# Order of layer 2's last block, place of a Tanh, ties and weight sums in a four-layer graph kernel

## The chip, the cores and the metric

The kernel runs on one core of one Trainium2 chip. The metric is the device time of one execution in microseconds (us). Three executions were timed, and the median is quoted; one more was profiled.

## What is computed

128 graphs of 64 nodes with 512 features pass four layers; after each, the input is added and the rows are normalised. Everything is 32-bit float. The reference, cut to what matters:

```
# layer 0: hypergraph convolution, twice (H = adj != 0)
h = relu(conv(x, adj, W1, b1)); h = layer_norm(h, gamma, beta); x = norm(x + conv(h, adj, W2, b2) + x)
# layer 1: attention from a sum of two scores
s = (x @ w) @ a
A = s[..., :, None] + s[..., None, :]
A = tanh(A / 8) * 8;  A = where(A >= 0, A, 0.1 * A);  A = exp(A) * adj
A = A / A.sum(-1) * adj.sum(-1);  x = norm(x + A @ x @ w)
# layer 2: three graph convolutions
h = relu(adj @ (x @ W1) + b1); h = relu(adj @ (h @ W2) + b2); x = norm(x + adj @ (h @ W3) + b3)
# layer 3: attention with 8 heads, adjacency and distance terms, output projection
attn = softmax(q k^T * scale) * 0.33 + 0.33 * adj + 0.33 * exp(-adj)
x = norm(x + (attn @ v) @ W_out + b_out)
```

## The kernel before

**Groups and steps.** The graphs are cut into 16 groups of 8 (512 rows: four pairs of graphs, 128 rows each). Three streams of work run at once. In step s, stream "a" does layers 0 and 1 of group s (`first_half`), stream "b" layer 2 and the first part of layer 3 of group s-1 (`second_half`), and stream "t" the rest of layer 3 of group s-2. Group 0 has its own code for layers 0 and 1 (`first_group`). Three strings, `order`, `step_1` and `step_last`, name the pieces of one step in the order in which they are written down: `b.l2c1` is the piece of stream b up to the `yield "l2c1"`. Steps 2 to 15 use `order`. From that sequence a scheduler sets the order of the instructions on each engine; it may move them, except where `behind(key)` ties an instruction after one that was remembered in `last_add` under that key (`tc.issue_after`), or where an engine is strict (the start, and the end).

**One multiplication.** `multiply` (L546) computes a 512x512 by 512x512 product with seven products of quarter blocks instead of eight. Each is one call of `product`: four matmul instructions of 128x256 (eight rows of the trace), twice that where two left sides are added. They run with the weights B11, T1, T2, B21, T3, B22, T4, where T1 to T4 are sums and differences of weight blocks (L263 to L268). There are three PSUM accumulators. `a_` takes B11, T2, T3 and T4; between them its contents are copied out by `snap` (L555): u1 after B11, u2 after T2. `b_` takes T1 (copied as u5) and B22. `c_` takes B21 alone. VectorE then adds: c + u1 (L575), a after T3 + u5 (L581), b after B22 + u2 (L590). T4 may write `a_` only when L581 has read it; T3 only when u2 has been copied. The last quarter is copied after T4 (L600, or L602 with a residual). The copies of u run on ScalarE, or on VectorE with a residual (`res`). `stops` says after which products the piece ends.

**Layer 2's last block.** Stream b's third multiplication has the key `l2c_q`, its result is g; 16 matmuls `agg` (L1145) follow, which need all of g, and VectorE adds them to x (L1151). Two of its adds are tied by `held`: c + u1 behind `e_(q+1)` and b + u2 behind `t_(q+1)`, both of layer 1.

**Layer 1's attention weights** run beside it, for group q+1: VectorE makes the scores (L815), transposes them (L620, L624), adds (L822, key `e`); ScalarE does Tanh (L825), VectorE the leaky part (L826), ScalarE Exp (L827), VectorE two products (L829, L830), the sum and its reciprocal (L834, L835), the same transposes again, and the last product (L838, key `t`). Tanh needs another table of functions than the root before it, so a table load stands ahead of it in ScalarE's order. `graph_T` then multiplies t with x (`gt_l`, L481), and two engines or ScalarE alone (`both`) copy the result out (L490, L492) for layer 1's multiplication `l1w`, whose T1 needs a sum of it, `s_l` (L518).

**The projection** of stream t has the key `wo_q` and a residual: pieces o1 (B11), o2 (T1), o3 (T2), and the rest. In o2 and o3 it is tied behind products 5 and 7 of `l2c_(q+1)`.

**Weights.** A ring of 20 tiles is filled by DMAs on SP's queue some 20 products ahead. For group 0 the sums T1 to T4 of a weight are made on VectorE (`making`, `make_half` for two parts of it) and stored by POOL's queue for the later groups.

Of the kernel before, what the change touches and what calls it, by code (L numbers as in the profile page):

```python
# [8 lines left out]
FP = mybir.dt.float32  # L9
# [32 lines left out]
def kernel(  # L42
# [455 lines left out]
    def newest(engine):  # L498
        return next(i for i in reversed(nc.cur_bb.bb.instructions) if i.engine == engine)

    def behind(key):
        return tc.issue_after(last_add[key]) if key in last_add else nullcontext()
# [25 lines left out]
    def product(acc, lefts, wt_q, what, first, last, flipped):  # L528
        ws = stream.take(*wt_q, what)
        n_k = 2 * len(lefts)  # L530
        for blk in range(2):
            for i in range(n_k):
                left, wt = lefts[i // 2].left[what][:, i % 2], ws[i // 2][:, i % 2]
                if flipped:
                    lhsT, rhs = wt[:, blk * P : (blk + 1) * P], left
                else:
                    lhsT, rhs = left[:, blk * P : (blk + 1) * P], wt

                ten.matmul(  # L539
                    acc[:, blk, :], lhsT, rhs,  # L540
                    start=(first and blk == 0 and i == 0), stop=(last and i == n_k - 1),
                    skip_group_check=True,
                )
        stream.done(*wt_q, what)

    def multiply(lefts, wt_q, dst, key, flipped=False, res=None, stops=(3,), then=None, held={}):  # L546

        acc = [ps_acc.tile([P, 2, Q], FP, name=f"{n}_{key}", tag="acc") for n in "ab"]

        def snap(ps, m, n, what):
            t = work.tile([P, 2, Q], FP, name=f"{what}_{key}", tag="w")
            last_add[f"{key}.{what}"] = (act.copy(t, ps) if res is None else vec.tensor_add(t, ps, res(m, n))).ins  # L555
            return t

        pa, pc = acc
        product(pa, lefts, wt_q, B11, True, False, flipped)
        s1 = snap(pa, 0, 0, "u1")  # L560
        if 1 in stops:
            yield
        product(pc, lefts, wt_q, T1, True, False, flipped)
        s5 = snap(pc, 1, 1, "u5")
        if 2 in stops:
            yield
        product(pa, lefts, wt_q, T2, False, False, flipped)
        s2 = snap(pa, 0, 1, "u2")
        last_add[f"{key}.p3"] = newest(PE)
        if 3 in stops:  # L570
            yield
        pb = ps_acc.tile([P, 2, Q], FP, name=f"c_{key}", tag="acc")
        product(pb, lefts, wt_q, B21, True, True, flipped)
        with behind(held.get(4)):
            vec.tensor_add(dst(0, 0), pb, s1)  # L575
        if then:
            then(0, 0, dst(0, 0))
        if 4 in stops:
            yield
        product(pa, lefts, wt_q, T3, False, False, flipped)  # L580
        last_add[f"{key}.d"] = vec.tensor_add(dst(1, 1), pa, s5).ins  # L581
        if then:
            then(1, 1, dst(1, 1))
        last_add[f"{key}.p5"] = newest(PE)
        if 5 in stops:
            yield
        product(pc, lefts, wt_q, B22, False, True, flipped)
        last_add[f"{key}.p6"] = newest(PE)
        with behind(held.get(6)):
            last_add[key] = vec.tensor_add(dst(0, 1), pc, s2).ins  # L590
        if then:
            then(0, 1, dst(0, 1))
        if 6 in stops:
            yield
        product(pa, lefts, wt_q, T4, False, True, flipped)
        last_add[f"{key}.p7"] = newest(PE)
        if then:
            then(1, 0, pa)
        elif res is None:
            act.copy(dst(1, 0), pa)  # L600
        else:
            vec.tensor_add(dst(1, 0), pa, res(1, 0))  # L602

    def whole(gen):
        for _ in gen:
            pass

    def nat(t):

        return lambda m, n: t[:, 2 * m : 2 * m + 2, n * Q : (n + 1) * Q]  # L610
# [130 lines left out]
    def first_half(g):  # L741
# [65 lines left out]
        next(gen)  # L807
        yield "w21"
        whole(gen)
        layer_norm(xg, f"l0_{q}")  # L810

        s4 = small.tile([P, G], FP, name=f"s4_{q}", tag="s4")
# [8 lines left out]
        t = grp.tile([P, G, C], FP, name=f"t_{q}", tag="t", bufs=1)  # L821
        last_add[f"e_{q}"] = vec.tensor_add(t, e, bcast(s4, G)).ins  # L822
        yield "w2"
        with behind("l2c_0.u2") if q == 1 else nullcontext():
            act.activation(t, t, AF.Tanh, scale=0.125)  # L825
        vec.scalar_tensor_tensor(t, t, 0.1, t, ALU.mult, ALU.max)  # L826
        last_add[f"exp_{q}"] = act.activation(t, t, AF.Exp, scale=8.0).ins  # L827
# [12 lines left out]
        left = Left(f"l1_{q}")  # L840
        for duo in range(2):
            with behind("agg_0.p") if q == 1 else nullcontext():
                graph_T(pair, t, left.t, duo, f"l1_{q}", both=q > 1)
        yield "c3"
        with behind(f"wo_{q - 2}"):
            left.sums()
# [216 lines left out]
    def second_half(g):  # L1063
# [26 lines left out]
        h1.sums()  # L1090
        yield "l2a"
        g2 = big.tile([P, G, D], FP, name=f"g2_{q}", tag="big")
        for _ in multiply([h1], (w_g[1], q), nat(g2), f"l2b_{q}"):
            yield "l2b1"
        yield "l2b"
        adt = grp.tile([P, G, C], FP, name=f"adt_{q}", tag="adt", bufs=1)
# [27 lines left out]
        if not alone:  # L1124
# [1 line left out]
        h2.sums()  # L1126
        yield "gh"
        g3 = big.tile([P, G, D], FP, name=f"g3_{q}", tag="big")
        gen = multiply([h2], (w_g[2], q), nat(g3), f"l2c_{q}", stops=(3, 5),
            held={4: f"e_{q + 1}", 6: f"t_{q + 1}"})  # L1130
        next(gen)
        yield "l2c1"
        next(gen)
        yield "l2c2"
        whole(gen)
        yield "l2c"
        for duo in range(2):

# [68 lines left out]
        left.sums()  # L1207
        yield "osum"
        gen = multiply([left], (w_o, q), nat(xg), f"wo_{q}", res=nat(xg), stops=(1, 2, 3))
        next(gen)  # L1210
        yield "o1"
        for n in range(2):
            with behind(f"l2c_{q + 1}.p{5 + 2 * n}"):
                next(gen)
            yield f"o{n + 2}"
        whole(gen)
        yield "o"
        with behind(f"q_{q + 1}"):
# [166 lines left out]
    def taken(duo, ps, left):  # L1385
# [11 lines left out]
    """.split()  # L1397
    order = """
        t.v1 a.c1 t.v b.gt t.soft a.w1a1 a.w1a t.soft2 a.resid b.l2a1 b.l2a a.w1b1 t.ptp a.w1b t.pv a.lnh b.l2b1
        t.osum a.c2a b.l2b a.c2b b.gb3 load a.w21 b.gh a.w2 rows b.l2c1 b.l2c2 a.ss a.den b.l2c t.o1 t.o2 t.o3 a.c3 b.agg rows2 t.o  # L1400
        rows3 a.p1 b.xT a.p2 b.q1 a.ln1 b.q t.ln3 b.k1 prep b.k b.dots
    """.split()

    step_1 = """
        b.l2a1 b.l2a a.lnh b.l2b1 a.c2a b.l2b a.c2b b.gb3 load a.w21 b.gh a.w2 rows b.l2c1 b.l2c2 a.ss a.den sumsq b.l2c b.agg
        sumsq2 a.c3 a.p1 b.xT sumsk a.p2 b.q1 a.ln1 b.q rows2 b.k1 b.k prep b.dots
    """.split()

    step_last = """
        t.v1 b.gt t.v t.soft t.soft2 b.l2a1 t.ptp b.l2a t.pv t.osum b.l2b1 b.l2b b.gb3 b.gh b.l2c1 b.l2c2 b.l2c t.o1 b.agg  # L1410
        t.o2 t.o3 t.o b.xT b.q1 b.q t.ln3 b.k1 b.k b.dots
    """.split()
    rest_last = "t.v1 t.v2 t.v t.pv0 t.o1 t.pv1 t.o".split()
    orders = {1: step_1, NGRP: step_last, NGRP + 1: rest_last}
# [43 lines left out]
    for n, (who, q, name) in enumerate(todo):  # L1458
        if n == n_start:
            strict.clear()  # L1460
        if n == n_end:
            strict.update((PE, DVE))
        if who == "load":
            if q > 1:
                groups[q] = load_group(q)
        elif who == "rows":
            if q > 0:
                preps[q] = prepare(groups[q])
            with behind(f"l0w2_{q - 1}.d") if q > 1 else nullcontext():
                next(preps[q])  # L1470
        elif who in ("prep", "rows2", "rows3"):
            next(preps[q])
        elif who == "doubled":
            doubled(groups[q])
        elif who == "constant":
            constant(groups[q])
        elif who == "keep":
            wt = (*w_1, w_2, w_l1)[q]
            stream.keep(wt)
        elif who == "wa":  # L1480
            if isinstance(wa_parts, tuple):
                wa_parts = make_wa(*wa_parts)
                vec.tensor_copy(mcol, mcol8)
                vec.tensor_copy(mi, mi8)
            else:
                spread_wa(wa_parts)
        elif who == "rest":
            with in_turn(SP, POOL):
                wa_parts = load_wa()
                b2_bc = load_row(b2, D, "b2_bc")  # L1490
                groups[1] = load_group(1)
                load_atx(first)
                load_masks(first)
                load_masks_cols()
                gb1_col = load_col(gb1, KD, "gb1_col")
                gb2_col = load_col(gb2, KD, "gb2_col")
                gb3_bc = load_row(gb3, D, "gb3_bc")
                bo_bc = load_row(bout, D, "bo_bc")
        elif who in ("sumsq", "sumsq2"):
            stream.make_half(w_q)  # L1500
        elif who == "sumsk":
            stream.make(w_k, 0)
        elif who == "bw":
            next(bw_parts)
        else:
            side = "a" if who == "a" else "b"
            if (side, q) not in gens:
                gens[side, q] = (second_half if side == "b" else first_half if q > 0 else first_group)(groups[q])
            did = next(gens[side, q])
            assert did == name, (did, name)  # L1510
# [55 lines left out]
```

## Time and profile before

| | |
|---|---|
| median of 3 executions | 2749.85 us (2749.43 to 2751.62) |
| the profiled execution | 2749.3 us |
| its span, first to last instruction | 2747.5 us |
| mean granted TensorE clock | 0.999 |
| one step, from 692.24 to 861.00 (third a_l2c product) | 168.76 us |
| DMA, share of 16 engines, main queue | 47.5% |
| ScalarE's table loads for Tanh, each | 1.28 us |
| add on VectorE of 128x512 (L575 and the like) | 0.68 us, the next one starts 0.60 later |
| copy on ScalarE of 128x512 (L555) | 0.57 to 0.59 us |

The span of the profile is one execution from its first to its last instruction; the execution's own time is 1.8 us longer. In a line of the timeline stand the start and the duration in us, the engine (PE is TensorE, DVE is VectorE, ACT is ScalarE), the line of the kernel, the operation, what it writes and reads (names of tiles without numbers, so that `u_l2c` stands for u1, u5 and u2), and in brackets how long the engine was idle before it and what released it. The end of a matmul is modelled, so successive starts say more than durations.

### The profile page before, as it was taken

The page shows a single profiled execution, that of the slowest core. Times are in us where ns is not written, and L with a number is a line of the kernel's source. Part 1 is how long each engine was busy: PE and PEld are TensorE (multiplying, and loading weights), DVE is VectorE, ACT ScalarE, POOL GpSimd, SP SyncE. Part 2 cuts the span into 40 slices and gives each one's busy share as a digit, 9 for nine tenths or more (in the row PEclk, how much of TensorE's full clock was granted, in tenths as well). Part 3 has the DMA queues.
Part 4 walks back from the last instruction along what each step waited for, and adds up shares of the span by engine and source line. Part 5 has one row for each costly group of instructions (what it writes and reads, how often), then busy time and mean ns, then how long its engine had stood idle before and what let it go on. Part 6 is the DMA issues. An engine that isn't in the chain of part 4 may idle for free.

```text
span 2747.5 us, 67717 instructions
## 1 busy us (share of the span) xinstructions
PE 2722.5 (99%) x28770; PEld 2347.5 (85%) x28770; DVE 2079.6 (76%) x4117; ACT 803.3 (29%) x1444; POOL 38.1 (1%) x71
## 2 busy tenths in 40 slices
PE   9999999999999999999999999999999999999998
PEld 7878888888888888888888888888888888888887
DVE  6878687776877778777786877778777687776766
ACT  3323323233232322322223232232322323232232
POOL 2000000000000000000000000000000000000000
PEclk9999999999999999999999999999999999999999
DMA  8535454454544545445454454545545455454441
GB/s 264 179 107 164 129 166 140 141 165 131 171 132 138 167 132 165 131 143 167 130 167 131 143 165 131 165 126 153 159 131 170 129 159 147 130 163 132 151 124 61
DMA packets 309388, 405.14 MB, mean 147 GB/s; under 512 B 57408, under 2 KB 185184, under 8 KB 309088
## 3 DMA queue, kind: packets, MB, share of 16 engines
q1 hardware_dynamic: 304256, 385.58, 47.5%
q0 software_dynamic: 4832, 15.24, 1.5%
q8 instruction: 228, 3.74, 0.6%
q14 instruction: 72, 0.59, 0.1%
HBM read 369.78 MB, written 30.93 MB: 146 GB/s over the span
## 4 chain that ended last, share of the span: by engine, by line
PE 88%; DVE 10%; ACT 1%; issue 1%; POOL 0%; DVEq 0%; POOLq 0%
PE a_l0w L539 13%; PE b_l0w L539 7%; PE a_l2b L539 4%; PE a_q L539 4%; PE a_k L539 4%; PE a_l2a L539 4%; PE a_v L539 4%; PE c_l0w L539 4%; PE a_l1w L539 4%; PE gt_l L481 3%; PE a_wo L539 3%; PE gt_l0h L481 2%; PE a_l2c L539 2%; PE b_l2b L539 2%; PE b_q L539 2%; PE b_k L539 2%
## 5 line engine op out<-in xcount | busy, mean ns | idle before, releaser
L539 PE MATMUL a_l0w<-w2w,aT_l0h 128*128 128x256 f32 x720 | 164.3, 381 | 0.0
L457 DVE BATCH_NORM_STATS2 st_l<-x 128x6 f32<-128x512 f32 x244 | 157.4, 671 | 0.6
L539 PEld LDWEIGHTS a_l0w<-w2w,aT_l0h 128*128 128x128 f32 x720 | 135.6, 190 | 18.8
L463 DVE TENSOR_SCALAR x<-x,mv_l,rs_l 128x512 f32<-128x512 f32 x244 | 119.2, 541 | 2.2
L539 PE MATMUL b_l0w<-w2w,s_l0h 128*128 128x256 f32 x480 | 108.5, 379 | 0.0
L771 ACT ACTIVATE h<-h 128x1024 f32<-128x1024 f32 (+1 forms) x58 | 54.9, 947 | 178.5 <-DVE h L590 157.5
L539 PEld LDWEIGHTS b_l0w<-w2w,s_l0h 128*128 128x128 f32 x480 | 91.1, 190 | 12.5
L1120 ACT ACTIVATE aT_h<-gth,gb_col 128x256 f32<-128x256 f32 x128 | 48.4, 489 | 159.0 <-PE gth L1112 159.0
L492 ACT COPY aT_l<-gt_l 128x512 f32<-128x512 f32 x148 | 78.1, 597 | 56.8 <-PE gt_l L481 56.8
L447 ACT ACTIVATE rs_l<-mv_l,eps_t 128x4 f32<-128x4 f32 (+1 forms) x64 | 19.0, 297 | 255.9 <-DVE mv_l L458 244.2
L555 DVE TENSOR_TENSOR u_l0w<-a_l0w,b_bc 128x512 f32<-128x512 f32 x56 | 38.6, 688 | 69.3 <-PE a_l0w L539 69.3
L539 PE MATMUL a_l2c<-gwcw,aT_h 128*128 128x256 f32 x360 | 86.7, 384 | 4.2 <-ACT u_l2c L555 3.2
L539 PE MATMUL a_l2b<-gwbw,aT_h 128*128 128x256 f32 x360 | 86.6, 383 | 0.7 <-ACT aT_oT L1388 0.7
L539 PE MATMUL a_q<-aT_xT,wqw 128*128 128x256 f32 x360 | 85.1, 379 | 0.6 <-ACT aT_xT L1170 0.6
L539 PE MATMUL a_l1w<-ww,aT_l 128*128 128x256 f32 x360 | 85.1, 379 | 0.2 <-ACT aT_l L492 0.2
L539 PE MATMUL a_k<-aT_xT,wkw 128*128 128x256 f32 x360 | 85.0, 379 | 0.0
L539 PE MATMUL a_l2a<-aT_l,gwaw 128*128 128x256 f32 x360 | 85.0, 379 | 0.0
L539 PEld LDWEIGHTS a_l2c<-gwcw,aT_h 128*128 128x128 f32 x360 | 67.0, 190 | 18.7 <-ACT u_l2c L555 8.7
L539 PE MATMUL a_v<-wvw,aT_xT 128*128 128x256 f32 x336 | 80.8, 383 | 0.0
L539 PE MATMUL a_l0w<-w1aw,aT_l 128*128 128x256 f32 x336 | 80.8, 383 | 0.0
L539 PE MATMUL a_wo<-wow,aT_oT 128*128 128x256 f32 x336 | 79.5, 379 | 0.1
L539 PE MATMUL a_l0w<-w1bw,aT_l 128*128 128x256 f32 x336 | 79.4, 379 | 0.0
(528 smaller groups left out, 6486.9 us busy)
## 6 DMA issues: line engine op xcount, KB each, us to landing
w2w<-w2k SPq DMA_DIRECT2D x210, 256.0 KB, 2.6
x<-in_x_dram SPq DMA_DIRECT2D x15, 1024.0 KB, 9.8
w1aw<-w1ak SPq DMA_DIRECT2D x60, 256.0 KB, 2.7
w1bw<-w1bk SPq DMA_DIRECT2D x60, 256.0 KB, 2.7
ww<-wk SPq DMA_DIRECT2D x60, 256.0 KB, 2.8
gwaw<-gwak SPq DMA_DIRECT2D x60, 256.0 KB, 3.1
gwbw<-gwbk SPq DMA_DIRECT2D x60, 256.0 KB, 2.6
gwcw<-gwck SPq DMA_DIRECT2D x60, 256.0 KB, 2.7
```

What stands on the lines that cost most here:

```text
L447: act.activation(rs[:, at], mv[:, at, 1], AF.Sqrt, bias=eps_t)
L457: vec.bn_stats(st, xg[:, p, :])
L463: vec.tensor_scalar(xg[:, p, :], xg[:, p, :], mv[:, p, 0:1], rs[:, p : p + 1], ALU.subtract, ALU.mult)
L481: ten.matmul(ps[g][f * C : (f + 1) * C, c, p, :], src(2 * duo + p)[rows, c0 : c0 + C], mat[rows, 2 * duo + p, :], start=True, stop=True,)
L492: act.copy(o[:, :, :, g, :], ps[g])
L539: ten.matmul(acc[:, blk, :], lhsT, rhs, start=(first and blk == 0 and i == 0), stop=(last and i == n_k - 1), skip_group_check=True,)
L555: last_add[f"{key}.{what}"] = (act.copy(t, ps) if res is None else vec.tensor_add(t, ps, res(m, n))).ins
L771: act.activation(hn, hn, AF.Relu)
L1120: act.activation(o[:, :, h, :], ps[h][:, c].rearrange("p (d a) i -> p d (a i)", d=2), AF.Relu, bias=gb2_col[:, k : k + 1],)
```

## The change

- `multiply` gets `early`: the product B21, its add and what follows are moved ahead of T1. It is used for layer 2's second multiplication of group 0 alone.
- Tanh is tied behind u2 of `l2c_(q-1)` for every group, not for group 1 alone.
- gt_l's copies go to both engines in group 1, too.
- `l2c` stops after product 6 instead of 5; its T4 is tied behind the projection's T1 (`wo_(q-1).p2`). The projection's three pieces are tied behind products 3, 6 and 7 of `l2c_(q+1)`. Their places in `order` and `step_last` move with them.
- For group 0's third multiplication (in step 1) both ties of `held` go.
- The sums of the projection's weights are made in two parts, in step 2: one ahead of layer 0's last norm, one behind the attention weights. In step 1, the second part of q's weight sums moves behind gt_l.

```diff
-    def multiply(lefts, wt_q, dst, key, flipped=False, res=None, stops=(3,), then=None, held={}):
+    def multiply(lefts, wt_q, dst, key, flipped=False, res=None, stops=(3,), then=None, held={}, early=False):
...
+        def first_quadrant():
+            pb = ps_acc.tile([P, 2, Q], FP, name=f"c_{key}", tag="acc")
+            product(pb, lefts, wt_q, B21, True, True, flipped)
+            with behind(held.get(4)):
+                vec.tensor_add(dst(0, 0), pb, s1)
+            if then:
+                then(0, 0, dst(0, 0))
+
+        if early:
+            first_quadrant()
         product(pc, lefts, wt_q, T1, True, False, flipped)
         s5 = snap(pc, 1, 1, "u5")
+        last_add[f"{key}.p2"] = newest(PE)
...
-        pb = ps_acc.tile([P, 2, Q], FP, name=f"c_{key}", tag="acc")
-        product(pb, lefts, wt_q, B21, True, True, flipped)
-        with behind(held.get(4)):
-            vec.tensor_add(dst(0, 0), pb, s1)
-        if then:
-            then(0, 0, dst(0, 0))
+        if not early:
+            first_quadrant()
...
         whole(gen)
+        if q == 2:
+            stream.make_half(w_o)
         layer_norm(xg, f"l0_{q}")
...
-        with behind("l2c_0.u2") if q == 1 else nullcontext():
+        with behind(f"l2c_{q - 1}.u2"):
             act.activation(t, t, AF.Tanh, scale=0.125)
...
-                graph_T(pair, t, left.t, duo, f"l1_{q}", both=q > 1)
+                graph_T(pair, t, left.t, duo, f"l1_{q}", both=True)
...
-        for _ in multiply([h1], (w_g[1], q), nat(g2), f"l2b_{q}"):
+        for _ in multiply([h1], (w_g[1], q), nat(g2), f"l2b_{q}", early=q == 0):
...
-        gen = multiply([h2], (w_g[2], q), nat(g3), f"l2c_{q}", stops=(3, 5),
-            held={4: f"e_{q + 1}", 6: f"t_{q + 1}"})
+        gen = multiply([h2], (w_g[2], q), nat(g3), f"l2c_{q}", stops=(3, 6),
+            held={4: f"e_{q + 1}", 6: f"t_{q + 1}"} if q > 0 else {})
         next(gen)
         yield "l2c1"
         next(gen)
         yield "l2c2"
-        whole(gen)
+        with behind(f"wo_{q - 1}.p2"):
+            whole(gen)
...
-        next(gen)
-        yield "o1"
-        for n in range(2):
-            with behind(f"l2c_{q + 1}.p{5 + 2 * n}"):
+        for n, p in enumerate((3, 6, 7)):
+            with behind(f"l2c_{q + 1}.p{p}"):
                 next(gen)
-            yield f"o{n + 2}"
+            yield f"o{n + 1}"
...
 (order)
-   ... a.ss a.den b.l2c t.o1 t.o2 t.o3 a.c3 b.agg rows2 t.o
+   ... a.ss a.den sumso t.o1 t.o2 b.l2c t.o3 a.c3 b.agg rows2 t.o
 (step_1)
-   ... sumsq b.l2c b.agg sumsq2 a.c3 a.p1 ...
+   ... sumsq b.l2c b.agg a.c3 sumsq2 a.p1 ...
 (step_last)
-   ... b.l2c1 b.l2c2 b.l2c t.o1 b.agg t.o2 t.o3 t.o ...
+   ... b.l2c1 b.l2c2 t.o1 b.l2c t.o2 b.agg t.o3 t.o ...
...
+        elif who == "sumso":
+            if q == 3:
+                stream.make_half(w_o)
```

`make_half(w_o)` makes T1 and T2 at its first call and T3 and T4 at its second (with the stores on POOL's queue).

## The prediction

> **What bounds the kernel now.** I read the engine shares of the page first, then the waits of TensorE, then the timeline of one steady step and of steps 1, 2 and 16.
>
> ```profile
> PE 2722.5 (99%) x28770; PEld 2347.5 (85%) x28770; DVE 2079.6 (76%) x4117; ACT 803.3 (29%) x1444; POOL 38.1 (1%) x71
> ...
> PE a_l2c L539 <- ACT u_l2c L555: 3.2, 13, 0.3
> PE agg L1145 <- DVE g L590: 2.8, 1, 2.8
> PE a_l2c L539 <- DVE g L581: 1.5, 2, 1.0
> ```
>
> TensorE has work for 99% of the span, so only its gaps, and nothing on another engine by itself, can be won. The waits (total us, times, longest) put the largest sum on one place that comes back 13 times: the fifth-in-line product of layer 2's third multiplication waits for a ScalarE copy. The other two lines belong to steps 1 and 2 alone. Step 3 (layer 0/1 of group 3, layer 2 of group 2, projection of group 1) shows the 13-fold one; columns are start, duration, engine, line, operation:
>
> ```profile
> 516.97 1.28 ACT L825 ACT_TABLE_LOAD   x1
> 519.62 1.89 PE L539 MATMUL a_l2c<-gwcw,s_h 128*128 128x256 f32 x8
> 521.34 1.89 PE L539 MATMUL b_l2c<-gwcw,s_h 128*128 128x256 f32 x8
> 522.07 0.42 DVE L822 TENSOR_TENSOR t<-e,s 128x256 f32<-128x256 f32 x1
> 522.53 0.42 ACT L825 ACTIVATE t<-t 128x256 f32<-128x256 f32 x1 [4.28 <-DVE t L822]
> 522.86 0.57 ACT L555 COPY u_l2c<-a_l2c 128x512 f32<-128x512 f32 x1
> 523.47 1.99 PE L539 MATMUL a_l2c<-gwcw,aT_h 128*128 128x256 f32 x8 [0.24 <-ACT u_l2c L555]
> 525.30 1.46 PE L539 MATMUL b_wo<-wow,s_oT 128*128 128x256 f32 x6
> ```
>
> The reader is to see that T2 (519.62) was over at 521.35, but its copy u2 stands behind the Tanh, which waits until 522.5 for VectorE; T3 writes the same accumulator and waits for u2. The end of a matmul is modelled, so I take starts. A product of 8 matmuls lasts 1.73 us from start to start. T3 was due at 521.34 + 1.73 = 523.07 and started at 523.47: 0.40 lost, more than the 0.24 shown; 525.30 - 523.47 = 1.83 adds another 0.10 that a product has whenever its start was held. Step 2 already has Tanh behind u2:
>
> ```profile
> 350.01 1.89 PE L539 MATMUL a_l2c<-gwcw,s_h 128*128 128x256 f32 x8
> 351.74 1.03 PE L539 MATMUL b_l2c<-gwcw,s_h 128*128 128x256 f32 x4
> 351.94 0.58 ACT L555 COPY u_l2c<-a_l2c 128x512 f32<-128x512 f32 x1 [4.38 <-PE a_l2c L539]
> 352.60 1.97 PE L539 MATMUL a_l2c<-gwcw,aT_h 128*128 128x256 f32 x8
> ```
>
> There u2 starts 0.20 after T2's successor and T3 starts 2.59 after T2, with only half of B22 (4 matmuls, 0.86) between: 1.73 + 0.86 = 2.59, no loss.
>
> **What the Trainium skill says.** "TensorE: Matmul & The Clock Gate", section on the 16 sub-arrays: VectorE and ScalarE queues are strict FIFO, TensorE's can only pull weight loads ahead. The trace agrees: u2 waited behind Tanh with its data ready for over 1 us. "ScalarE: Activation LUTs", What ACT_TABLE_LOAD costs: about 1283 ns for the load and 1380 ns more for a drain. The trace has 1.28 us for the load; in step 1 a root (L447) starts at 209.55 behind a load of 208.25 to 209.53, so I count no drain after it. This matters because the load moves with Tanh.
>
> **The change part by part.** The profiled execution took 2749.3 us (span 2747.5 and 1.8 around it); the median of the runs is 2749.85, 0.55 higher.
>
> *Steps 3 to 15, Tanh and the new order (13 times).* The changed program's instruction order in each: B11, T1, B21, T2, half of B22, T3, other half, projection B11 and T1, T4, projection T2, then gt_l. Ten products as before, none added. Before: 512.71 to gt_l at 530.58 is 17.87 = 10 x 1.727 + 0.40 + 0.10 + 0.10 at the change to small matmuls. Replayed: T2 517.89, u2 519.82 to 520.40, T3 due 520.48. Step 2 gives 2.59 from T2 to T3, step 1 (185.63 to 188.25) 2.62, so 0.00 to 0.03 is lost where 0.40 was; the 0.10 stays. gt_l comes at 530.18. What else could be late: T4 (526.6) needs g's add of T3, which VectorE does at 523.4; projection T1 needs the buffer that the first g add frees at 523.0; projection T2 (528.35) needs u_wo, done at 526.75. gt_l needs t. VectorE's order now has all three g adds and two u_wo ahead of t's last product: t 522.07, g 522.42, t 523.02, g 523.36, Exp done 523.9, tn 524.0, g 524.33, t 524.93, sum and reciprocal to 525.77, transpose 526.1, u_wo to 526.75, transposes to 528.0, u_wo 528.6, t done at 529.0. That is 1.2 before gt_l. The table load, now 520.4 to 521.7, is done before t arrives at 522.4; with the page's drain Tanh would start at 523.1, 0.6 later, inside the 1.2. ScalarE has nothing else there. Weight loads are issued over 30 us ahead of use (the last of gwcw at 489.10 for T4 at 526.60); on SP's queue only adn moves ahead of two wqw loads, which are used 30 us later. Nothing. Sum: 13 x 0.40 = 5.2 (4.8 to 5.5).
>
> All times are on the clock of the execution before, so later steps don't carry the shift of earlier ones.
>
> *Step 1, layer 2's second multiplication with B21 early.* Before, T1 of l2b_0 waited for s_h: 139.17 instead of 138.54, plus 0.10. B21 needs neither s_h nor the last relu, takes that place, and T1 comes at 140.28 with s_h ready at 139.0. Saved 0.70 (0.4 to 0.8).
>
> *Step 1, no ties, gt_l copies shared, weight sums moved.*
>
> ```profile
> 190.56 0.41 DVE L826 SCALAR_TENSOR_TENSOR t<-t 128x256 f32<-128x256 f32 x1
> 190.90 0.68 DVE L581 TENSOR_TENSOR g<-a_l2c,u_l2c 128x512 f32<-128x512 f32 x1
> 191.63 1.99 PE L539 MATMUL a_l2c<-gwct,aT_h 128*128 128x256 f32 x8 [0.53 <-DVE g L581]
> 195.66 0.68 DVE L590 TENSOR_TENSOR g<-b_l2c,u_l2c 128x512 f32<-128x512 f32 x1
> 196.40 0.64 PE L1145 MATMUL agg<-g,atc 64*64 64x512 f32 x1 [2.77 <-DVE g L590]
> ```
>
> In the new order the first g add goes ahead of e's transposes, which delays t and everything behind it on VectorE by 0.6: the add of T3 comes at 191.5, T4 at 192.24 (0.6 worse). The add of B22 now stands right behind tn, at 192.4, so agg starts when T4 is through, at 194.2 (2.2 better), and gt_l at 197.2. But VectorE is full: t done at 196.2, a weight sum, agg's add, a weight sum, three more adds to 199.8, two gt_l copies (0.6 each, ScalarE's before) to 201.05, two weight sums to 202.25, then s_l. l1w's T1 needs s_l: in step 1 the start of such a sum to T1 is 0.84 (138.33 to 139.17), so T1 at 203.1 against 203.94. Of 2.8 only 0.84 remains (bounds 0.1 and 2.2). Step 1 in all: 1.5.
>
> *Step 2, w_o's sums in parts, new order.* Before, l2c to gt_l was 361.82 - 343.11 = 18.71, with T4 held until 356.44 and gt_l by 0.33. Now T4 runs at 357.02 behind both projection products and its add is done by 355.6; gt_l is due at 360.58. Two of the four sums go into layer 0's norm and end by 345.5; they move the norm by 0.05. The t chain is 1.24 later than in step 3 (its t at 353.71), so t ends at about 360.75: gt_l 0.2 late. Then the other two sums (1.2) stand ahead of u_wo and the gt_l copies on VectorE, the first copy starts at 362.45, agg's second tile at 363.1 against 363.74. Gain 0.6 (0.3 to 1.2).
>
> *Step 16.* Projection B11 and T1 stand around T4, agg is 1.73 later, and the norm of group 15 follows it. T3 of the projection waits for u_wo until 2675.04 (0.1 lost, before 0.2); the last three normalisations end at 2680.95, the second half of xtp is due at 2680.97. Gain 0.1 (-0.6 to 0.2).
>
> Sum: 5.2 + 1.5 + 0.6 + 0.1 = 7.4: 2749.3 - 7.4 = 2741.9 in a profiled execution, 2742.4 on the scale of the median (-0.27%).
>
> **Rivals.** About 0.2%, 5.5 us, is what can be told from no change.
> A, forecast: the replay holds; own range 5.7 to 9.3 won, 2740.5 to 2744.2.
> B, half won: u2 with only 0.86 of cover misses it by a little in the steady steps (0.15 of 0.40, because u2 ended at 352.52 for a T3 at 352.60, 0.08 in hand), and VectorE gives nothing back in steps 1 and 2: 13 x 0.25 + 0.7 = 4.0, 2745.9. For it: the thin 0.08. Against: two steps show the same spacing with at most 0.03 lost.
> C, more: steps 1 and 2 keep nearly all their waits (2.2 + 0.7 + 1.2) with 5.5 in the steady steps: 9.6, 2740.2. Against: VectorE's queue counted above.
> D, slower: t takes over as what ends last. It has 1.2 in hand ahead of gt_l; from 1.6 beyond the replay the steady gain is gone, and each further us costs 13. With t 2.4 late (the drain and a second VectorE stall of 1.8): 13 x 0.8 - 2.2 = 8.2 lost, 2758. For it: three adds and two u_wo in its chain. Against: each has a measured 0.6, and the replay includes them. That the change does nothing is out: the instruction order shows it.
>
> **Chances.** A 0.72, B 0.16, C 0.08, D 0.04. A is the time. A little of A is below 5.5, nearly all of B is: faster 0.78, same 0.18, slower 0.04. The range takes in C and B: 2739 to 2746.
>
> **What would show it.** No wait of a_l2c for u_l2c above 0.05 in steps 3 to 15, a step of 168.36 instead of 168.76, no wait of gt_l for t there; in step 1 a longer wait of T4 (about 1.1), none of agg, and one of b_l1w for s_l; in step 2 a short one of gt_l for t. Waits of gt_l for t in every step would make it wrong towards D, a step of 168.5 or more towards B.

## The result, and the profile after

The changed kernel takes 2742.20 us (median of 8 executions, 2741.53 to 2744.82), the kernel before 2749.86 beside it: ratio 0.9974, 95% interval 0.9965 to 0.9983. A second comparison gave 2742.40 against 2749.72, ratio 0.9973 (0.9963 to 0.9984). 2742.4 was forecast. The profiled execution has a span of 2739.8, 7.7 less than before. All times are in us.

The engine shares of the page say the same as before, TensorE is busy for 99%:

```profile
PE 2720.2 (99%) x28770; PEld 2348.2 (86%) x28770; DVE 2079.1 (76%) x4119; ACT 804.2 (29%) x1442; POOL 38.0 (1%) x71
```

The waits of TensorE (us in total, times, longest) no longer hold the line of a_l2c for u_l2c, 3.2 in 13 waits before. Agg's wait of 2.8 is gone too. New is the one of a_l1w:

```profile
PE a_l1w L539 <- issue: 2.1, 1, 2.1
...
PE a_l2c L539 <- DVE g L589: 1.0, 1, 1.0
...
PE gt_l L481 <- DVE t L848: 0.4, 2, 0.3
```

Step 3 in the timeline of the changed kernel (start, duration, engine, line, operation, what ended the idle time before it):

```profile
516.40 1.89 PE L539 MATMUL a_l2c<-gwcw,s_h 128*128 128x256 f32 x8
518.12 1.03 PE L539 MATMUL b_l2c<-gwcw,s_h 128*128 128x256 f32 x4
518.32 0.59 ACT L555 COPY u_l2c<-a_l2c 128x512 f32<-128x512 f32 x1 [2.87 <-PE a_l2c L539]
518.93 1.28 ACT L835 ACT_TABLE_LOAD   x1
...
518.99 1.97 PE L539 MATMUL a_l2c<-gwcw,aT_h 128*128 128x256 f32 x8
...
521.04 0.42 ACT L835 ACTIVATE t<-t 128x256 f32<-128x256 f32 x1 [0.83 <-DVE t L832]
```

u2 follows T2 at once, T3 starts 2.59 after T2, and the table load and Tanh come behind. T3 of the next step starts at 687.31: a step takes 168.32 where it took 168.76.

Step 1 is where the profile departs from the forecast:

```profile
191.17 1.99 PE L539 MATMUL a_l2c<-gwct,aT_h 128*128 128x256 f32 x8 [0.98 <-DVE g L589]
...
193.09 0.64 PE L1156 MATMUL agg<-g,atc 64*64 64x512 f32 x1
...
195.20 2.10 PE L481 MATMUL gt_l<-t,x 64*64 64x64 f32 x128 [0.16 <-DVE t L848]
...
198.66 1.28 DVE L490 COPY aT_l<-gt_l 128x512 f32<-128x512 f32 x2
199.45 2.52 PE L539 MATMUL a_l1w<-ww,aT_l 128*128 128x256 f32 x8 [2.15 <-issue]
...
201.06 0.69 DVE L518 TENSOR_TENSOR s_l<-aT_l 128x512 f32<-128x512 f32 x1
...
201.85 3.09 PE L539 MATMUL b_l1w<-ww,s_l 128*128 128x256 f32 x8
...
204.78 1.89 PE L539 MATMUL a_l1w<-ww,s_l 128*128 128x256 f32 x8
```

gt_l starts 4.19 earlier than before (199.39), but TensorE then stands still for 2.15, and T1 of l1w_1 lasts 2.93 from start to start where such a product takes 1.73. The windows view (stretch, its length, busy time and instructions of PE, PEld, DVE, ACT, POOL, the granted clock, DMA share, GB/s) tells why, first of the changed kernel, then of the kernel before:

```profile
196.00:199.40 3.40, 1.30 (x91) 1.16 (x80) 3.40 (x7) 1.17 (x2) 1.08 (x2) 1.00 0.68 211
199.40:202.00 2.60, 2.55 (x9) 1.79 (x10) 2.57 (x5) 0.00 (x0) 1.08 (x2) 0.75 0.90 248
202.00:204.80 2.80, 2.80 (x9) 2.25 (x10) 2.80 (x6) 0.59 (x1) 0.00 (x0) 0.62 0.86 303
```

```profile
193.40:196.40 3.00, 0.23 (x3) 0.01 (x1) 2.90 (x8) 0.58 (x1) 0.36 (x1) 1.00 0.10 22
196.40:199.40 3.00, 3.00 (x17) 0.95 (x21) 1.83 (x3) 0.00 (x0) 0.72 (x2) 0.59 0.46 175
199.40:202.10 2.70, 2.47 (x132) 2.33 (x124) 2.43 (x4) 1.12 (x3) 0.25 (x1) 0.83 0.08 18
```

The reader is to see the clock (third number from the end): behind an idle stretch it falls below 1.00 in both kernels. The trace's records of it show one stretch of 3.413 at exactly half, from 200.72 in the changed kernel, from 196.92 before. Before, it fell on agg and gt_l (agg to gt_l 2.99, in the changed kernel 2.11); now it falls on two dense products.

The lead of the changed kernel at the same TensorE instruction, the two profiles laid side by side, grows like this:

| where | forecast | measured |
|---|---|---|
| program start | - | 0.22 |
| step 1, l2b_0 with B21 early | 0.70 | 0.69 |
| step 1, from l2c_0 to T2 of l1w_1 | 0.84 | -0.02 |
| step 2 | 0.6 | 0.60 |
| steps 3 to 15 | 13 x 0.40 = 5.2 | 13 x 0.437 = 5.68 |
| a pause inside gt_l near 1264, in the profile of before alone | - | 0.50 |
| step 16 | 0.1 | 0.10 |
| sum | 7.4 | 7.77 |

### The profile page after: what moved, and what is told of

Its sections match the earlier page's. It is cut to its first block, busy times and chain, and to the rows that moved or that the text cites. A ratio compares the mean times of both kernels' runs of the same rounds, so it can differ in the third digit from the quotient of the medians.

```text
span 2739.8 us, 67717 instructions
## 1 busy us (share of the span) xinstructions
PE 2720.2 (99%) x28770; PEld 2348.2 (86%) x28770; DVE 2079.1 (76%) x4119; ACT 804.2 (29%) x1442; POOL 38.0 (1%) x71
## 4 chain that ended last, share of the span: by engine, by line
PE 95%; DVE 3%; ACT 1%; issue 0%; DMA 0%; POOL 0%; DVEq 0%; POOLq 0%
PE a_l0w L539 15%; PE b_l0w L539 7%; PE a_l2b L539 4%; PE a_q L539 4%; PE a_k L539 4%; PE a_l2a L539 4%; PE a_v L539 4%; PE c_l0w L539 4%; PE a_l1w L539 4%; PE a_wo L539 4%; PE a_l2c L539 4%; PE gt_l L481 3%; PE gt_l0h L481 2%; PE b_l1w L539 2%; PE b_l2a L539 2%; PE b_l2b L539 2%
## 5 line engine op out<-in xcount | busy, mean ns | idle before, releaser
L539 PEld LDWEIGHTS a_l1w<-ww,aT_l 128*128 128x128 f32 x360 | 68.5, 190 | 11.6 <-issue 2.3
```

Of the source, the lines that this page charges most:

```text
L539: ten.matmul(acc[:, blk, :], lhsT, rhs, start=(first and blk == 0 and i == 0), stop=(last and i == n_k - 1), skip_group_check=True,)
```

## The experiments

Each run was timed beside the kernel before. The kernel before had medians of 2749.15 to 2749.86 in these comparisons, so a difference of under some 0.7 between medians of two rows says little. For step 1 they say less than one distance in the profile: from B11 of l2b_0 to group 2's `sps` products (some 100 later, with the same TensorE work in all but the two filled kernels). What is lost at the start itself is not in it. Here are all profiles:

| kernel | B11 of l2b_0 to sps | half clock in step 1 | median |
|---|---|---|---|
| before | 104.16 | yes | 2749.86 |
| changed | 103.48 | yes | 2742.20 |
| changed, again | 103.38 | yes | 2742.40 |
| tie of Tanh only, on the kernel before | 104.20 | yes | 2746.55 |
| product order only | 103.36 | yes | 2762.10 |
| step 1 as before | 101.41 | no | 2740.73 |
| q's sums later | 101.28 | no | 2742.56 |
| ties back | 101.90 | no | 2741.43 |
| gt_l copies on ScalarE | 101.16 | no | 2740.75 |
| idle stretch filled, three times | 104.06 | no | 2744.25 |
| idle stretch filled, once | 102.35 | no | 2743.50 |
| w_o's sums in one part | 103.51 | yes | 2743.38 |
| step 1 put together | 99.46 | no | 2738.58 |
| the same, again | 99.45 | no | 2739.83 |

**The tie alone**, on the kernel before:

```diff
-        with behind("l2c_0.u2") if q == 1 else nullcontext():
+        with behind(f"l2c_{q - 1}.u2"):
```

> The kernel before with one edit: Tanh is tied behind u2 in every group, not only in group 1; product order, ties and sums stay as before. Theory 1 (the stall only moves): the old order puts T4 right behind the second half of layer 2's B22, and T4 needs VectorE's add of T3. In step 3 of the kernel before, T2 at 519.62 gives T3 at 522.21 (0.4 + no wait), but Tanh now comes behind u2 and its table load, at about 523.4, the add of T3 stands behind the t product that follows it, ends near 525.0, and T4, due at 522.21 + 1.73 + 0.86 = 524.80, starts near 525.2. So 0.40 won at T3 and about 0.40 lost at T4: 2749.9, within 1.5 either way, with a wait of a_l2c for the g add in steps 3 to 15 and none for u_l2c. Theory 2 (the tie is what pays): the 13 x 0.40 to 0.44 go with the tie alone, 2744.2 to 2744.7, no new wait.

Measured 2746.55 (12 executions), ratio 0.9989 (0.9981 to 0.9998): 3.0 won, between the two theories. Step 3 of this kernel's timeline:

```profile
522.19 1.28 ACT L825 ACT_TABLE_LOAD   x1
522.25 1.97 PE L539 MATMUL a_l2c<-gwcw,aT_h 128*128 128x256 f32 x8
...
523.48 0.42 ACT L825 ACTIVATE t<-t 128x256 f32<-128x256 f32 x1
...
524.28 0.68 DVE L581 TENSOR_TENSOR g<-a_l2c,u_l2c 128x512 f32<-128x512 f32 x1
...
525.01 1.99 PE L539 MATMUL a_l2c<-gwcw,aT_h 128*128 128x256 f32 x8
```

T3 (522.25) has lost its wait. T4 was due at 522.25 + 1.73 + 0.86 = 524.84 and starts at 525.01, held by the add of T3 at 524.28. So about half of the gain is handed on: the lead over the kernel before grows by 0.23 a step, 13 x 0.23 = 3.0 (two steps in which this profile pauses inside gt_l left out). I had T4 at 525.2; it comes 0.2 earlier, and 0.2 a step is what remains of the gain. Tanh starts 0.01 after the end of its table load (522.19 + 1.28), so the further drain that the prediction allowed for does not show here.

**The product order alone**, the same line turned back in the changed kernel:

```diff
-        with behind(f"l2c_{q - 1}.u2"):
+        with behind("l2c_0.u2") if q == 1 else nullcontext():
```

> The changed kernel with one edit: Tanh is tied behind u2 in group 1 only, as before; the new product order stays. Theory 1: order and tie only work together. Tanh waits for t until 521.04 in step 3 of the changed kernel, u2 then runs from 521.5 to 522.05, T3 starts near 522.1 where it could have started at 520.7 behind T2, B22 and half a projection product: 1.4 lost plus 0.1 for a held start, in 13 steps: 13 x 1.5 = 19.5 slower than the changed kernel, about 2761.7 (2757 to 2765), 12 slower than before. Theory 2: the new order alone carries the gain (T2 stands 1.73 earlier in it): no more than 2744. Step 1 is the same as in the changed kernel, so it also gives a second look at where the half clock falls there.

Measured 2762.10 (4 executions), ratio 1.0045 (1.0029 to 1.0062), 12.6 slower than the 2749.51 of before beside it: theory 1. Step 3 and the waits of this kernel:

```profile
521.76 1.03 PE L539 MATMUL a_wo<-wow,aT_oT 128*128 128x256 f32 x4
...
522.95 0.42 ACT L835 ACTIVATE t<-t 128x256 f32<-128x256 f32 x1 [4.28 <-DVE t L832]
523.27 0.57 ACT L555 COPY u_l2c<-a_l2c 128x512 f32<-128x512 f32 x1
...
523.89 1.99 PE L539 MATMUL a_l2c<-gwcw,aT_h 128*128 128x256 f32 x8 [1.11 <-ACT u_l2c L555]
```

```profile
PE a_l2c L539 <- ACT u_l2c L555: 16.7, 14, 2.3
```

u2's data has been there since about 520 (T2 starts at 518.30), it stands behind Tanh, and T3 waits for it. A step loses 1.30 against the changed kernel, less than the 1.5 expected. The fourteenth wait, 2.3, is step 2's, which the expectation had left out: without a tie Tanh comes ahead of u2 there too (1.8 lost). Each half alone pays 3.0 or costs 12.6; together they win 5.7 in these steps. The tie is what clears T3; the order gives T4 room. Which part of the order does that (the projection's products ahead of T4, the earlier add of B22) was not separated.

**Step 1 as before**, all else changed:

```diff
-        for _ in multiply([h1], (w_g[1], q), nat(g2), f"l2b_{q}", early=q == 0):
+        for _ in multiply([h1], (w_g[1], q), nat(g2), f"l2b_{q}", early=False):
-            held={4: f"e_{q + 1}", 6: f"t_{q + 1}"} if q > 0 else {})
+            held={4: f"e_{q + 1}", 6: f"t_{q + 1}"})
-                graph_T(pair, t, left.t, duo, f"l1_{q}", both=True)
+                graph_T(pair, t, left.t, duo, f"l1_{q}", both=q > 1)
 (step_1)
-   ... a.c3 sumsq2 a.p1 ...
+   ... sumsq2 a.c3 a.p1 ...
```

> The changed kernel with step 1 as before: B21 of l2b_0 not early, the two ties of group 0's g adds, gt_l copies of group 1 on ScalarE alone, the weight sums at their old place. Steps 2 to 16 stay changed. Theory 1 (ledger of the two traces): step 1 is worth 0.70 (l2b_0) + 0.0 (l2c_0 to l1w_1), so 2742.9. Theory 2 (the prediction's sum): 0.70 + 0.84 = 1.54, so 2743.7. The start of T2 of l1w_1, measured from the start of l2b_0's B11, tells them apart better than the time: the same as in the changed kernel plus 0.7, or plus 1.5.

Measured 2740.73 (2740.33 to 2741.21), 1.5 faster than the changed kernel: both theories fall. The step-1 edits as a whole cost time, although B21 early, one of them, won 0.7. In the timeline of this run, too, VectorE does the add of B22 0.93 behind that of T3, ahead of t's last steps, and agg starts 5.31 after T3 of l2c_0, not 8.15 as before. The ties are back here, so leaving them out is not what makes this add early. By the code it comes from `stops=(3, 6)`: the add is now written down in the piece l2c2, ahead of a.den, when `last_add` does not hold `t_1` yet, and `behind` then ties nothing. In the changed kernel the second tie of `held` is dead in all groups; "ties back" brings back the first alone. This run:

```profile
191.62 0.68 DVE L589 TENSOR_TENSOR g<-a_l2c,u_l2c 128x512 f32<-128x512 f32 x1
...
192.55 0.68 DVE L598 TENSOR_TENSOR g<-b_l2c,u_l2c 128x512 f32<-128x512 f32 x1
...
194.28 0.64 PE L1156 MATMUL agg<-g,atc 64*64 64x512 f32 x1
...
196.39 2.10 PE L481 MATMUL gt_l<-t,x 64*64 64x64 f32 x128 [0.16 <-DVE t L848]
...
198.73 1.99 PE L539 MATMUL a_l1w<-ww,aT_l 128*128 128x256 f32 x8 [0.24 <-ACT aT_l L492]
...
201.05 0.68 DVE L518 TENSOR_TENSOR s_l<-aT_l 128x512 f32<-128x512 f32 x1
...
201.83 1.97 PE L539 MATMUL b_l1w<-ww,s_l 128*128 128x256 f32 x8 [1.11 <-issue]
```

B11 starts 2.34 after gt_l, in the changed kernel 4.25 after it.

**The parts of step 1, one at a time.** First q's sums behind the first products of l1w_1:

```diff
 (step_1)
-   ... a.c3 sumsq2 a.p1 ...
+   ... a.c3 a.p1 sumsq2 ...
```

> The changed kernel with one edit: in step 1 the second half of w_q's sums stands behind the first five products of l1w_1, so that s_l follows the gt_l copies at once (at about 199.95 instead of 201.06 in the changed kernel's profile). Theory 1 (the half clock sets T1 there): B11 still runs slow after an idle stretch of 2.15, T1 of l1w_1 stays at 201.85 (within 0.15) and the whole changes by less than 0.3: 2742.2. Theory 2 (s_l sets T1): T1 comes 0.65 earlier, at 201.2, and the time falls to 2741.5.

```profile
200.74 1.97 PE L539 MATMUL a_l1w<-ww,aT_l 128*128 128x256 f32 x8 [2.15 <-issue]
...
201.34 0.69 DVE L518 TENSOR_TENSOR s_l<-aT_l 128x512 f32<-128x512 f32 x1
...
202.54 1.89 PE L539 MATMUL b_l1w<-ww,s_l 128*128 128x256 f32 x8
```

The same 2.15 of idle time, but no half clock in this execution: B11 to T1 takes 1.80. T3 of l2c_0 to T1 of l1w_1 is 13.90, in the changed kernel 14.51: theory 2's 0.6. Another 0.4 is won behind T2, in the products of q and k. But no half clock fell here, so this profile can't refute theory 1: in the two in which it began soonest behind B11 (product order only; changed, again) T1 came 15.12 and 15.16 after T3, so there the slow B11 set it, and not s_l. The median, 2742.56, shows no gain.

The ties (in effect the first one) back:

```diff
-            held={4: f"e_{q + 1}", 6: f"t_{q + 1}"} if q > 0 else {})
+            held={4: f"e_{q + 1}", 6: f"t_{q + 1}"})
```

> The changed kernel with one edit: the two ties of group 0's g adds are back, so that VectorE does the first g add behind t's sum, not ahead of e's transposes. The prediction costed going without them at 0.6 worse for T4 of l2c_0 and at nothing afterwards, since VectorE's queue holds the same work. Theory 1: nothing afterwards is wrong too: without ties VectorE stands idle 0.48 waiting for Tanh, with them it does the add in that time; T3 of l2c_0 to gt_l is 7.42 with ties (the run with step 1 as before) and 7.86 without (the changed kernel), so everything from T4 to l1w_1 comes 0.44 earlier: 2741.8. Theory 2 (the prediction): T4 earlier, T1 of l1w_1 at the same distance from l2c_0's T3 as in the changed kernel where no half clock falls: 2742.2.

Measured 2741.43 (2740.16 to 2742.87). T3 to gt_l is 7.41 instead of 7.86: theory 1.

All gt_l copies of group 1 on ScalarE:

```diff
-                graph_T(pair, t, left.t, duo, f"l1_{q}", both=True)
+                graph_T(pair, t, left.t, duo, f"l1_{q}", both=q > 1)
```

> The changed kernel with one edit: group 1's gt_l copies are all on ScalarE again. Theory 1: the shared copies are what turned the gain of step 1 into nothing: VectorE is full, so the copy that B11 of l1w_1 needs comes only behind agg's adds (B11 at 199.45), while ScalarE would do it by about 197.5. B11 then at 197.6, TensorE's idle stretch ahead of it near 0.3, no half clock; T1 waits for s_l, which starts 1.2 earlier, at 199.9: T1 at 200.7. Together 1.2 for T1 and 0.6 for the half clock of every second run: 2740.4. Theory 2 (sharing helped as the prediction's edit list has it, two engines copy faster than one): s_l comes no earlier and the time is 2742.2 or more.

```profile
196.62 2.05 ACT L492 COPY aT_l<-gt_l 128x512 f32<-128x512 f32 x4 [2.63 <-PE gt_l L481]
...
197.75 1.99 PE L539 MATMUL a_l1w<-ww,aT_l 128*128 128x256 f32 x8 [0.24 <-ACT aT_l L492]
...
200.07 0.68 DVE L518 TENSOR_TENSOR s_l<-aT_l 128x512 f32<-128x512 f32 x1
...
200.85 1.97 PE L539 MATMUL b_l1w<-ww,s_l 128*128 128x256 f32 x8 [1.11 <-issue]
```

Measured 2740.75 (2739.86 to 2741.78), times and places as theory 1 has them. ScalarE does all four copies in 2.05; VectorE started its first at 198.66, behind agg's adds. Sharing put the copy that B11 needs on the engine that was full.

**The half clock.** To shorten the idle stretch without moving anything else, `graph_T` repeated matmuls of gt_l's second tile, with the same results:

```diff
+        for _ in range(again):
+            for c in range(4):
+                for p in range(2):
+                    for f in range(2):
+                        c0 = c * P + f * C
+                        ten.matmul(
+                            ps[1][f * C : (f + 1) * C, c, p, :], src(2 * duo + p)[C:, c0 : c0 + C],
+                            mat[C:, 2 * duo + p, :], start=True, stop=True,
+                        )
...
-                graph_T(pair, t, left.t, duo, f"l1_{q}", both=True)
+                graph_T(pair, t, left.t, duo, f"l1_{q}", both=True, again=3 if q == 1 and duo == 1 else 0)
```

> The changed kernel with work added: in group 1 the 16 matmuls of gt_l's second tile are done three times more, with the same results, in the idle stretch of TensorE ahead of l1w_1 (2.15 long). They last about 0.8 (128 of them take 2.1) and end before VectorE copies that tile. Theory 1 (the clock is halved for one window of 3.413 when TensorE was busy for less than some 0.4 of the window before; the windows run from the release of the clock at the start, so that the phase differs between executions): no window falls under 0.58, so no execution shows a half clock in step 1 (mean clock 1.0 in all, where half of the changed kernel's runs have 0.999), B11 to T2 of l1w_1 is about 4.1 (B11 at 1.9 to 2.4 ahead of T1, which waits for s_l) where it was 5.33 in the changed kernel's profile, and the median falls by about 0.6, to 2741.6. Theory 2 (the stretch has nothing to do with idle time): half of the runs still show 0.999 and the time stays.

A miss: 2744.25. Three repetitions took 3.2, not 0.8, and B11 came at 201.99. With one (`again=1`):

> As the run that filled TensorE's idle stretch ahead of l1w_1, with one repetition in place of three (three took 3.2, four times what was estimated, because they use one half of the array's rows where gt_l uses both at once, and pushed B11 back by 2.5). One takes 1.1 and ends before VectorE starts the copies, so B11 and T1 stay where they are on the changed kernel's clock (B11 199.45, T1 201.85), the idle stretch falls to about 1.0, no window of 3.413 falls under 0.6 of busy time, T1 to T2 of l1w_1 is 1.8 (2.93 in the changed kernel's profile) and the median falls by about 0.6, to 2741.6. Theory 2 (idle time has nothing to do with it): a half-clock stretch in step 1 stays possible, and the time is 2742.2.

```profile
198.49 1.11 PE L492 MATMUL gt_l<-t,x 64*64 64x64 f32 x32
...
201.09 1.99 PE L548 MATMUL a_l1w<-ww,aT_l 128*128 128x256 f32 x8 [1.50 <-issue]
...
203.20 1.97 PE L548 MATMUL b_l1w<-ww,s_l 128*128 128x256 f32 x8
...
205.00 1.89 PE L548 MATMUL a_l1w<-ww,s_l 128*128 128x256 f32 x8
```

In the profile it is as theory 1 says: 14.51 from T3 of l2c_0 to T1, as in the changed kernel (B11 comes 0.29 later, but T1 does not wait for it), then 1.80 to T2 instead of 2.93, no half clock, 102.35 instead of 103.48. The median of 12, 2743.50, is 1.3 above the changed kernel, not 0.6 below. Part of that is known for the profiled execution: beside the changed kernel's profile it is 1.38 behind by 13.5 (0.49 of it ahead of the first matmul, the rest by a late release of the clock), and a gt_l of layer 0 paused for 1.07 near 2440. Whether this kernel has more such pauses as a rule is open.

The Trainium skill, "TensorE: Matmul & The Clock Gate", Part 1, says that the clock is gated to half or full in free-running windows of 3413 ns, to half after an idle window. The records agree in the ratio and the length: every half-clock stretch begins a whole number of windows of 3.413 after the clock's first release, in step 1 after 55 or 56 of them.

But a wholly idle window is not needed here. How idle it must be is read from the 14 profiles, with windows laid from the release on: 11 windows have TensorE busy for 0.19 to 0.39 of their length (6 in step 1, 5 near the end), and half clock follows each; so it does behind the almost empty ones at the very end. The lowest that none follows have 0.46, 0.46 and 0.51. In the changed kernel a window can hold 2.15 of idle time, which leaves 0.37, but only if it lies around it. With step 1's code of the changed kernel, the clock was released 3.8, 4.8, 3.8 and 4.8 after the first matmul in the four profiles with half clock; the two profiles with the same 2.15 of idle and no half clock (ties back, sums later) had 6.3 and 6.6. So in these six the place of the windows, which the release at the start sets, decides. And a late release costs about as much there: of the two profiles of the best version below, released 4.1 and 6.4 after the first matmul, the second is 1.02 behind by 14.8. These profiles of the changed step 1 pay at the one place or at the other.

The mean granted clock of nearly every timed execution is on record as well, to three digits. A whole stretch of 3.413 at half takes 1.7 of some 2740 away and leaves 0.9994, so an execution with 1.000 had none. One with 0.999 may have had it, or half clock in the last stage only, as the first profile of the best version did. The changed kernel has 1.000 in 7 of 15 executions, the kernel before in 41 of 84, the kernel filled once in 10 of 12; the two kernels of step 1 as before and copies on ScalarE, without a long idle stretch, in 11 of 11. So the same kernel runs with and without the half clock. The medians at 1.000 and at 0.999 are 2748.81 and 2749.88 for the kernel before, 2741.90 and 2742.59 for the changed one, which fits a price of about 1, though the release at the start is in them too. The kernel filled once got rid of most of its half clocks by this count and is slower all the same: its 10 executions at 1.000 have a median of 2743.49. That filling pays is therefore shown in the profile of step 1 only, not in the whole time.

**w_o's sums in one part:**

```diff
         if q == 2:
-            stream.make_half(w_o)
+            pass
...
             if q == 3:
-                stream.make_half(w_o)
+                pass
```

> The changed kernel with w_o's four weight sums in one part again, all inside layer 0's norm of step 2. Theory 1: the third and fourth sum (1.2) then stand ahead of t's chain, and gt_l, which already waits 0.28 for t in the changed kernel, starts 1.2 later, at about 361.2 instead of 360.0 on the clock of the changed kernel's profile; behind gt_l it wins back 0.2 at most since its copies on VectorE have two sums less ahead of them: 1.0 slower (0.6 to 1.3), 2743.2. Theory 2 (the sums are hidden wherever they stand): 2742.2 and no longer wait of gt_l.

Measured 2743.38 (2741.49 to 2743.84). In the profile three of the sums stand ahead of t's chain and the fourth inside it, gt_l starts 0.5 later than in the changed kernel (361.02, of whose 1.02 the start explains 0.5), and 0.2 remains behind it. Whether the 1.2 of the median comes from the sums isn't settled; the profile shows 0.2 of it.

**Step 1 put together:** early B21 and the new order stay, the first tie back, copies on ScalarE, q's sums later.

```diff
-                graph_T(pair, t, left.t, duo, f"l1_{q}", both=True)
+                graph_T(pair, t, left.t, duo, f"l1_{q}", both=q > 1)
...
-            held={4: f"e_{q + 1}", 6: f"t_{q + 1}"} if q > 0 else {})
+            held={4: f"e_{q + 1}", 6: f"t_{q + 1}"})
...
 (step_1)
-   ... a.c3 sumsq2 a.p1 ...
+   ... a.c3 a.p1 sumsq2 ...
```

> The changed kernel with step 1 put together from the parts that paid: B21 of l2b_0 early and the new product order stay; ties of group 0's g adds back; all gt_l copies of group 1 on ScalarE; the second half of w_q's sums behind the first five products of l1w_1. Theory 1: against the run with step 1 as before (2740.7) B21 early gives 0.7 and s_l, no longer behind two sums, about 1.1 (there T1 of l1w_1 waited 1.1 for it): 2738.9, no half clock in any run (the idle stretches are of about 1.1), T3 of l2c_0 to T2 of l1w_1 13.6 where it was 17.44 in the changed kernel. Theory 2: the sums are then late for group 0's projections to q, or another VectorE wait comes back, and it stays at 2740.0 or above.

Measured 2738.58 (2738.07 to 2739.81). Its step 1:

```profile
196.18 2.05 ACT L492 COPY aT_l<-gt_l 128x512 f32<-128x512 f32 x4 [2.63 <-PE gt_l L481]
...
197.31 1.99 PE L539 MATMUL a_l1w<-ww,aT_l 128*128 128x256 f32 x8 [0.24 <-ACT aT_l L492]
...
198.43 0.68 DVE L518 TENSOR_TENSOR s_l<-aT_l 128x512 f32<-128x512 f32 x1
...
199.21 1.96 PE L539 MATMUL b_l1w<-ww,s_l 128*128 128x256 f32 x8
...
201.01 1.89 PE L539 MATMUL a_l1w<-ww,s_l 128*128 128x256 f32 x8
```

No wait for s_l beyond 0.2, no half clock, T3 to T2 of l1w_1 13.46. Then both once more in one comparison:

> The changed kernel as it is, beside the next run, so that the two stand on the same chip: 2742.2 (within 0.7). Theory of the window: whether its profile shows a half-clock stretch in step 1 is decided by where the clock was released at the start; it shows one if a window of 3.413 counted from there has TensorE busy for under 0.4, and none otherwise.

> The version of step 1 put together from the parts that paid, a second time: 2738.6 (within 0.7), so 3.6 faster than the changed kernel in the same call. If the edits of step 1 in it were worth no more than the 0.7 that the prediction's sum would leave between the two, it would come out at 2741.5 or above.

Measured 2742.40 (2741.20 to 2744.22) and 2739.83 (2738.45 to 2740.28): 2.6, where 3.6 was expected (2739.83 lies outside the 0.7 given), and no execution of the one reaches the other in either comparison (15 of the changed kernel from 2741.20 up, 10 of this one to 2740.28). The changed kernel's profile had its half clock again, behind a window with 0.37 of busy time.

## Why the prediction was right, and where not

- **Steps 3 to 15**: right in the mechanism, 0.437 for 0.40, 5.68 in all. T2 to T3 is the 2.59 of the replay, t has about 1 in hand ahead of gt_l, no new wait. The two single runs show that the order had to come with the tie. The term was 0.04 a step too small: T3 to the product behind it is 1.80 now and was 1.83, where I had left all of the 0.10 behind a held start in place; that is 0.03 of it.
- **B21 early**: 0.69 for 0.70. **Step 2**: 0.60 for 0.6, with the short wait of gt_l for t (0.28) that was named. **Step 16**: 0.10 for 0.1.
- **Step 1 from l2c_0 on** is the term that failed: 0.84 ("of 2.8 only 0.84 remains"), measured -0.02. T4, agg and gt_l moved as forecast in kind (0.45 worse, 2.4 and 3.3 better), and VectorE's full queue held T1 of l1w_1 back, as the sum said: T1 had 1.18 of the lead left. It lost that in its own 2.93 at half clock. The step left out the clock. I read 2.77 of idle time and the durations behind it in the profile of before as the price of agg and gt_l, though a half-clock stretch lay on them (agg to gt_l 2.99 for 2.11, gt_l to B11 2.72 for 2.34, together 1.26), and didn't ask what 2.15 of idle time ahead of dense products would do. The wait named as a sign, of b_l1w for s_l, does not show; B11, ahead of it, stood still for 2.15 instead. And that agg comes early was right for another reason than the one I gave: the place where the add of B22 is written down, not the missing ties. The parts, from the distances in the table: new order of the tail 104.16 to 101.41 (1.26 of it is that stretch), early B21 -0.70, no first tie +0.45, shared copies +1.19 (101.90 against 101.16 less the 0.45), half clock +1.13 (103.48 against 102.35): 103.48.
- The sum came out because three errors nearly cancel, and that is luck: -0.86 in step 1, +0.48 in the steady steps, and +0.72 that has nothing to do with the change (start and pause). In medians: 7.66 for 7.4.
- **Rivals.** B (half won) is refuted by 13 steps without a wait. C's 2740.2 needed step 1's waits to be won; the edits there lost them again, and putting them right reached 2738.6 to 2739.8. D did not come: t was never late in these steps.
- Giving the ties no further cost was a second, smaller mistake: without the first tie VectorE stands idle for 0.48 waiting for Tanh.

## What to carry to other kernels

Where a copy waits behind another instruction in a strict queue, moving that instruction helps only if the work behind the freed one has room too: here the tie alone gave 3.0, the order alone cost 12.6, both gave 5.7. Don't move copies to the engine whose queue is full, even if two engines look faster than one. And before an idle stretch of over 2 us on TensorE is costed, look at the granted clock behind it in the windows view: the price is the gap plus up to half of the 3.4 at half clock (1.7; of which 1.13 and 1.26 were lost here), it falls on whatever stands there, and not every execution pays it.

## What was not expected of the hardware

- A gap of 2.15 is enough for 3.413 of half clock, if a window lies around it (0.19 to 0.39 busy: always, 0.46 and more: never, in 14 profiles). It happens in some executions of a kernel and not in others (7 of 15 of the changed kernel and 41 of 84 of the kernel before had none), and cost 1.1 to 1.3 in the profiles where it did (step 1 changed, step 1 before).
- Streams of small gt_l matmuls paused for 0.3 to 1.1 of idle time shown (0.5 and 1.3 lost) at a place that differs between executions (near 1264 in the profile of before, near 2440 in that of the kernel filled once), with no wait that the profile shows. A lead of some 0.5 in a single profile can be such a pause.
- Repeated 64x64 matmuls that use one half of the array's rows took 1.11 for 32, while 128 of gt_l, which alternate between the halves, take 2.1: twice as long for each.
